# Output blocks inside the arm of a switch, and half-empty blocks in two column tiles: a gated cross-attention and top-4-of-16 MoE kernel on one core

## The chip, the cores and the metric

The kernel runs on one core of a Trainium2 chip. The metric is the device time of one execution in microseconds (us); of several executions the median counts. Everything is computed in 32-bit floats, and a matrix product in this format is recorded as several passes of TensorE (PE). The other engines are VectorE (DVE), ScalarE (ACT), GpSimd (POOL) and the queue that starts most of the loads (SP).

## The reference, cut to what matters

```python
# x: 8 x 256 x 512, ctx: 8 x 256 x 512; LN is a layer norm over the last axis
s   = sigmoid(einsum('bdn,bdm->bnm', LN(x), ctx) / sqrt(256))
x   = x + tanh(g_xattn) * einsum('bvn,bnm->bvm', ctx, s)
xf  = LN(x).reshape(2048, 512)
t   = xf * rsqrt(mean(xf * xf, -1) + eps) * norm_w
vals, idx = top_k(t @ gate_w.T + gate_b, 4)          # 16 experts
G   = zeros(2048, 16); G[row, idx] = softmax(vals)
h   = einsum('mh,eoh->emo', t, w1) + b1              # 1024 outputs: a, b interleaved
a   = minimum(h[..., ::2], 7); b = clip(h[..., 1::2], -7, 7)
act = a * sigmoid(1.702 * a) * (b + 1)
y   = einsum('emi,edi->emd', act, w2) + b2
x   = x + tanh(g_ffn) * (xf + einsum('me,emd->md', G, y))
```

The reference computes all 16 experts for all rows; the kernel computes only the four that a row has chosen.

## The kernel before

The 2048 rows are 16 blocks of 128. The first part (to about 160 us) does attention, norms, the gate and the choice of experts, batch by batch; POOL writes each chosen pair (row, gate) into a table in DRAM, sorted by expert. The second part works on *chunks*: up to R = 4 blocks of 128 rows that all go to one expert. Two early chunks of three blocks (AHEAD) are done while the list of the others is still being built (to about 238 us), and then come the chunks of the list, 22 with these inputs, from 238.2 us to the last pass at 929.6 us.

The list is computed on DVE (lines 905 to 1021), one partition for each block of the list (partition q = 4 * chunk + block). `lim` (L973) is how many rows are left for that block, `full` masks the slots that hold one. `ids` and `gts` (row numbers and gates) are transposed on PE into the PSUM tile `pid` (L991, L992), and copied out as `idsG` (for gathering, L994), `idsT` (for adding to the output, L998; an empty slot gets a number past the last row and is dropped by the bounds check) and `gtsT` (L1000). `meta` holds for each chunk its size class, its number of blocks, its expert and whether it exists.

The order of the work in a chunk is written out by hand (`tc.manual_schedule`), and each engine runs its own instructions in that order. `chunk(c)` (L1108) does:

- POOL gathers the rows of the next chunk (`fetch`, L1037: four indirect loads into xg). The rows of this chunk are in xT already.
- A switch (L1118) over 17 row counts, 256 to 512 in steps of 16. Each of its arms holds `hidden` (L299) for that count: four groups of two PSUM tiles with four products each, recorded as 64 passes, with the row count as the moving size. PE fills `h0` to `h3` in turn (PSUM, four buffers); DVE reads each twice (L308, L317), ACT applies the activation (L316), DVE writes `act` (L325).
- SP loads the first weights of the chunk after the next two (w1r, 2 MB) once hidden has read its slot.
- `turn` (L284, L285): PE transposes the next chunk's rows, 16 passes into four PSUM tiles, and DVE multiplies them by the norm weight into xT.
- `expect` (L1061): PE, DVE and ACT read the next chunk's size class and give a hint at which arm comes next.
- `output` (L1079): block 0 always, blocks 1 to 3 each under an `If` on the number of blocks (L1087). A block is `combine` (L334: eight recorded passes of 512 columns into `h[k]`), the addition of the bias on DVE (L342, yb), the scaling with the gate on ACT (L347, yo), and on POOL an indirect DMA that adds the 128 rows to the output in DRAM (L351). Where a block does not exist, `skip` (L1066) issues four blank products of one column, so that both ways raise the same semaphores.
- SP loads the second weights (w2r) and the output bias (br).

So a chunk with 272 rows computes three full output blocks, though its last one holds 16 rows. The end of an arm (L1213 in the trace) is a jump to the code behind the switch; each arm gives a hint for it at its own start.

Of the kernel before, what the change touches and what calls it, by code (L numbers as in the profile page):

```python
# [31 lines left out]
def kernel(  # L32
# [35 lines left out]
    SIZES = list(range(2 * P, R * P + 1, GRAIN))  # L68
    ROWS = E * NT

    out_rows = out.rearrange("b d n -> (b d) n")

# [26 lines left out]
        "yb": (moe, [P, H], 2),  # L99
        "yo": (moe, [P, H], 3),  # L100
# [33 lines left out]
    blank = const.tile([P, P], mybir.dt.bfloat16, name="blank")  # L134
    nc.vector.memset(blank, 0.0)
# [10 lines left out]
    )  # L146
    eps = const.tile([P, 1], F32, name="eps")
# [69 lines left out]
    for tag in ("xT", "act"):  # L217
        nc.gpsimd.memset(buf(tag, 0), 0.0)
# [110 lines left out]
    def combine(slot, k, lo):  # L329

        py = buf("h", k)
# [9 lines left out]
        yb = buf("yb", k)  # L341
        nc.vector.tensor_tensor(yb, py, br[:, slot, :], ALU.add)  # L342
        return yb

    def scaled(k, yb, gate):
        y = buf("yo", k)
        nc.scalar.activation(y, yb, AF.Copy, scale=gate)  # L347
        return y

    def deliver(c, y, ids):  # L350
        put = nc.gpsimd.indirect_dma_start(  # L351
            out=out_rows,
# [4 lines left out]
            bounds_check=T - 1,  # L357
# [13 lines left out]
    with tc.tile_pool(name="att", bufs=2) as ap:  # L371
# [88 lines left out]
        def second_norm(b):  # L460
# [24 lines left out]
                else buf("yo", c)  # L485
# [267 lines left out]
        def output_early(a):  # L753
            pairs, target = early[a]
            ys = []
            for k in range(AHEAD):
                yb = combine(place_of(a - 2), k, k * P)
                ys.append(scaled(k, yb, pairs[:, k, 1:2]))
            early[a] = ys, target
# [169 lines left out]
    for h in range(2):  # L929
# [45 lines left out]
    )  # L975
    full = small("full", P, P)
# [13 lines left out]
    pid = ps_t.tile([P, 2, P], F32, tag="t", name="pid")  # L990
# [6 lines left out]
    idsT = small("idsT", P, P, dtype=I32)  # L997
    nc.vector.tensor_scalar(idsT, pid[:, 0, :], float(T), None, ALU.add)  # L998
    gtsT = small("gtsT", P, P)
    nc.vector.tensor_copy(gtsT, pid[:, 1, :])  # L1000


    meta = small("meta", P, 4, C1, dtype=I32)
# [9 lines left out]
    nc.vector.tensor_copy(meta[0:1, 1], blocks[0:1])  # L1013
    nc.vector.tensor_copy(meta[0:1, 2], expert[0:1])
    nc.vector.tensor_scalar(
        meta[0:1, 3], unit[0:1], ends[0:1, E - 1 : E], None, ALU.is_lt
# [7 lines left out]
    held_tiles["y"] = [  # L1024
# [7 lines left out]
    held_tiles["x"] = held_tiles["t"] + held_tiles["y"]  # L1032
# [30 lines left out]
    def skip(k):  # L1063

        for i in range(IC):
            nc.tensor.matmul(  # L1066
                buf("h", k)[:, 0:1],
                blank,
                blank[:, 0:1],
                start=True,  # L1070
                stop=True,
            )

    def output_block(c, k):
        q = c * R + k
        yb = combine(place_of(c), k, k * P)
        deliver(c, scaled(k, yb, gtsT[:, q : q + 1]), idsT[:, q : q + 1])

    def output(c):  # L1079


        blocks = read(meta[0:1, 1, c : c + 1], R)
        for k in range(R):
            if k == 0:
                output_block(c, k)
                continue
            with tc.If(blocks > k) as more:  # L1087
                output_block(c, k)
            with more.Else():
                skip(k)  # L1090


    begun = small("begun", P, 4, SLOTS, dtype=I32)
# [14 lines left out]
    def chunk(c):  # L1108
# [5 lines left out]
        e = read(meta[0:1, 2, c : c + 1], E - 1, [ET.DVE])  # L1114
# [102 lines left out]
```

## Time and profile before

| | |
|---|---|
| median of 3 runs | 946.06 us (941.92 to 950.2) |
| profiled execution, its own time | 949.47 us |
| its span | 947.9 us |
| mean granted clock of TensorE | 0.987 |
| 0 to 238 us: PE busy | 214.21 us |
| blocks of output in the list's chunks | 69, and 19 skipped |
| deliveries (L351), mean of one | 69, 1577 ns |

The span is the time from the first to the last instruction in the profile; the profiled execution's own time lies 1.6 us above it. A row of the table of stages has the stretch, its length, then for each engine its busy time and number of instructions, the granted clock, the share of busy DMA engines and GB/s. A row of the waits says which engine and line waited for which, how long in total, how often, and the longest. The chain of waits lists in order of time what ended last: start, length, what. A row of groups has the line, the engine, the operation, what it writes and reads, its shape and count; behind the bar the busy time and the mean of one in ns, the idle time before it and what ended that. A recorded pass lasts longer than the distance to the next one, since passes are pipelined: what a pass costs is read from the chain, as the length of a piece over its count.

### The profile page before, as it was taken

What the parts mean: (1) busy time and instruction counts of PE and PEld (TensorE: products, weight loads), DVE (VectorE), ACT (ScalarE), POOL (GpSimd) and SP (SyncE); (2) the same over time, 40 slices, a digit from 0 to 9 for tenths busy, and PEclk for the clock granted to TensorE, in tenths of its full rate; (3) what the DMA queues carried; (4) which work ended last, traced back from release to release, by engine and by line L of the source; (5) the groups of instructions that cost most, each with busy time, mean ns of one, the idle gap of its engine ahead of it and who ended that gap; (6) DMA issues with size and microseconds to landing.
All of it is one profiled execution on the core that took longest, in us unless ns stands there. A gap on an engine that the chain in (4) does not pass through costs nothing.

```text
span 947.9 us, 10767 instructions
## 1 busy us (share of the span) xinstructions
PE 902.0 (95%) x3134; PEld 524.3 (55%) x3134; DVE 386.1 (41%) x895; ACT 200.5 (21%) x319; POOL 287.6 (30%) x266
## 2 busy tenths in 40 slices
PE   5999995999999999999999999999999999999992
PEld 3455443555555555555444565666667677556760
DVE  3367565584333333333332333333333444333440
ACT  5567662411110110110111110111101111111110
POOL 3034445434230421421312421423213232313222
PEclk9999999999999999999999999999999999999996
DMA  5379942806864545646443654766457667634232
GB/s 170 115 160 166 164 98 69 287 7 154 294 164 159 136 122 167 168 127 192 133 118 117 180 180 128 191 208 187 164 185 216 186 177 210 207 116 123 66 71 32
DMA packets 42339, 144.77 MB, mean 153 GB/s; under 512 B 9569, under 2 KB 9697, under 8 KB 35521
## 3 DMA queue, kind: packets, MB, share of 16 engines
q1 hardware_dynamic: 20016, 98.58, 33.2%
q0 software_dynamic: 20896, 42.96, 20.7%
q8 instruction: 93, 1.52, 0.7%
q14 instruction: 198, 1.61, 0.5%
q10 hardware_dynamic: 1136, 0.10, 0.1%
HBM read 126.33 MB, written 28.38 MB: 163 GB/s over the span
## 4 chain that ended last, share of the span: by engine, by line
PE 60%; issue 14%; DMA 12%; DVE 6%; POOL 3%; ACT 2%; another core or an unknown queue 1%; POOLq 0%; DVEq 0%
PE ph L299 33%; PE ph L334 18%; DMA out_dram<-yo,idsT 11%; PE psc L434 3%; POOL out_dram L351 1%; PE pz L284 1%; PE pt L284 1%; PE pav L446 1%; DVE st L392 1%; DVE xs L453 1%; POOL xg L1037 1%; POOL table L638 1%; ACT xs L509 0%; DVE q L407 0%
## 5 line engine op out<-in xcount | busy, mean ns | idle before, releaser
L299 PE MATMUL ph<-xT,w1r 128*128 128x288 f32 (+10 forms) x1536 | 458.4, 459 | 7.9 <-DVE xT L285 4.7
L299 PEld LDWEIGHTS ph<-xT,w1r 128*128 128x128 f32 x1536 | 291.6, 191 | 166.3 <-issue 66.7
L334 PE MATMUL ph<-w2r,act 128*128 128x512 f32 x600 | 261.6, 592 | 0.6 <-issue 0.5
L351 POOL DMA_INDIRECT out_dram<-yo,idsT x69 | 108.8, 1577 | 461.4 <-ACT yo L347 446.2
L334 PEld LDWEIGHTS ph<-w2r,act 128*128 128x128 f32 x600 | 112.1, 190 | 133.1 <-issue 133.1
L316 ACT ACTIVATE ga<-ga 128x384 f32<-128x384 f32 (+10 forms) x96 | 47.3, 493 | 335.7 <-DVE ga L308 294.9
L317 DVE TENSOR_SCALAR v<-ph,bh 128x384 f32<-128x384 f32 (+10 forms) x96 | 55.6, 579 | 143.2 <-PE ph L299 134.4
L347 ACT ACTIVATE yo<-yb,gtsT 128x512 f32<-128x512 f32 x69 | 47.7, 717 | 293.4 <-DVE yb L342 284.0
L1037 POOL DMA_INDIRECT xg<-t_rows,idsG x92 | 90.7, 985 | 40.0 <-issue 23.0
L308 DVE TENSOR_SCALAR ga<-ph,bh 128x384 f32<-128x384 f32 (+10 forms) x96 | 55.6, 580 | 112.6 <-PE ph L299 83.8
L638 POOL DMA_INDIRECT table<-pair,sloti x64 | 62.5, 977 | 112.7 <-DVE mr L473 79.4
L342 DVE TENSOR_TENSOR yb<-ph,br 128x512 f32<-128x512 f32 x75 | 49.8, 686 | 67.5 <-PE ph L334 43.7
L285 DVE TENSOR_TENSOR xT<-pt,nw 128x512 f32<-128x512 f32 x46 | 29.6, 686 | 111.0 <-issue 97.5
L434 PE MATMUL psc<-kv,q 128*128 128x512 f32 x128 | 60.6, 621 | 2.4 <-ACT kvT L427 2.4
L446 PE MATMUL pav<-sc,kvT 128*128 128x512 f32 x128 | 58.7, 602 | 3.7 <-DVE mine L698 3.4
L325 DVE SCALAR_TENSOR_TENSOR act<-v,ga 128x384 f32<-128x384 f32 (+10 forms) x96 | 50.1, 522 | 14.2 <-ACT ga L316 4.6
L446 PEld LDWEIGHTS pav<-sc,kvT 128*128 128x128 f32 x128 | 23.2, 190 | 31.0 <-issue 26.5
L434 PEld LDWEIGHTS psc<-kv,q 128*128 128x128 f32 x128 | 24.4, 199 | 28.4 <-issue 24.8
L285 DVE TENSOR_TENSOR xT<-pz,nw 128x512 f32<-128x512 f32 x46 | 29.4, 681 | 0.0
L284 PEld LDWEIGHTS pt<-ident,xg 128*128 128x128 f32 x184 | 21.5, 141 | 5.8 <-issue 3.3
L284 PE MATMUL pz<-ident,xg 128*128 128x128 f32 x184 | 23.8, 273 | 0.0
L284 PE MATMUL pt<-ident,xg 128*128 128x128 f32 x184 | 23.8, 273 | 0.0
(177 smaller groups left out, 367.5 us busy)
## 6 DMA issues: line engine op xcount, KB each, us to landing
w1r<-in_L_ffn_w_dram SPq DMA_DIRECT2D x24, 2048.0 KB
w2r<-in_L_ffn_w_dram SPq DMA_DIRECT2D x27, 1024.0 KB
br<-in_L_ffn_b_dram SPq DMA_DIRECT2D x27, 256.0 KB
w1r<-in_L_ffn_w_dram SPq DMA_DIRECT2D x6, 1024.0 KB
xs<-in_x_dram SPq DMA_DIRECT2D x16, 256.0 KB
kv<-in_ctx_dram SPq DMA_DIRECT2D x16, 256.0 KB
out_dram<-xs SPq DMA_DIRECT2D x16, 256.0 KB
t_rows<-u SPq DMA_DIRECT2D x8, 256.0 KB
```

The source lines that it names most:

```text
L284: nc.tensor.transpose(px[:, h, :], xg[:, ts(h, P)], ident)
L285: nc.vector.tensor_tensor(buf("xT", 0)[:, :, lo : lo + P], px, nw.unsqueeze(2).to_broadcast([P, HC, P]), ALU.mult,)
L299: nc.tensor.matmul(ph[:, 0:n], w1r[:, slot, k, h, ts(i, P)], xT[:, k, lo : lo + n], start=(k == 0), stop=(k == HC - 1),)
L308: nc.vector.tensor_scalar(ga[:, 0:n], halves[0][:, 0:n], bias[:, 0, i : i + 1], LIMIT, ALU.add, ALU.min,)
L317: nc.vector.tensor_scalar(v[:, 0:n], halves[1][:, 0:n], bias[:, 1, i : i + 1], 1.0 + LIMIT, ALU.add, ALU.min,)
L325: nc.vector.scalar_tensor_tensor(act[:, i, lo : lo + n], v[:, 0:n], 1.0 - LIMIT, ga[:, 0:n], ALU.max, ALU.mult)
L334: nc.tensor.matmul(py, act[:, i, lo : lo + P], w2r[:, slot, i, :], start=(i == 0), stop=(i == IC - 1),)
L351: put = nc.gpsimd.indirect_dma_start(out=out_rows, out_offset=bass.IndirectOffsetOnAxis(ap=ids, axis=0), in_=y, in_offset=None, compute_op ...
L434: nc.tensor.matmul(ps, qs[b][:, c, ts(n, P)], kvs[b][:, c, :], start=(c == 0), stop=(c == DC - 1),)
L446: nc.tensor.matmul(po, kvTs[b][:, n, ts(c, P)], scs[b][:, n, :], start=(n == 0), stop=(n == NCH - 1),)
L638: put = nc.gpsimd.indirect_dma_start(out=table, out_offset=bass.IndirectOffsetOnAxis(ap=sloti[:, j : j + 1], axis=0), in_=pair[:, c, k, :] ...
L1037: nc.gpsimd.indirect_dma_start(out=buf("xg", k), out_offset=None, in_=t_rows, in_offset=bass.IndirectOffsetOnAxis(ap=idsG[:, q : q + 1], a ...
```

## The change

- The switch's arm now holds more. After hidden come the turn of the next chunk and then `output_rest`: the full blocks 2 and 3, as far as the arm's row count has them, and, if the count in halves of 64 rows is odd, a half block for the last one. Blank products fill up to the same number in every arm. The arm's size decides all of it, so the `If`s and `skip` are gone.
- The half block (`combine_half`) handles 64 rows of `act`. The same 64 rows are the weights of two column tiles: the first makes columns 0 to 255 in partitions 0 to 63, the second columns 256 to 511 in partitions 64 to 127. Its result `yh` (128 x 256) is added to the output seen as rows of half the length.
- After the arm: the load of w1r, the hint, the deliveries of blocks 2 and 3 and of the half block, always, with numbers past the end where there is nothing to add; then blocks 0 and 1 with their deliveries, always.
- The list gets `half` (at most 64 rows left in this block, and it is block 2 or 3), and from it `twice` (the first 64 numbers and gates, doubled), two more transposes into `pid`, `idsH` and `gtsH`; `idsT` leaves out the half blocks. `meta` loses the number of blocks.
- The result tiles `yb` (2) and `yo` (3) become `y` (4) and `yh` (1), scaled in place. `blank` is a view of `ones`.

```diff
@@ -66,9 +66,11 @@
 
     GRAIN = 16
     SIZES = list(range(2 * P, R * P + 1, GRAIN))
+    HALF = P // 2
     ROWS = E * NT
 
     out_rows = out.rearrange("b d n -> (b d) n")
+    out_halves = out.rearrange("b d (g n) -> (b d g) n", g=2)
 
     const = ctx.enter_context(tc.tile_pool(name="const", bufs=1))
     ring = ctx.enter_context(tc.tile_pool(name="ring", bufs=1))
...
@@ -96,8 +98,8 @@
         "act": (moe, [P, IC, R * P], 1),
         "ga": (moe, [P, R * P], 2),
         "v": (moe, [P, R * P], 2),
-        "yb": (moe, [P, H], 2),
-        "yo": (moe, [P, H], 3),
+        "y": (moe, [P, H], R),
+        "yh": (moe, [P, H // 2], 1),
     }
     held_tiles = {
         tag: [pool.tile(shape, F32, name=f"{tag}{i}") for i in range(n)]
...
@@ -131,8 +133,8 @@
     make_identity(nc, ident)
     ones = const.tile([P, P], F32, name="ones")
     nc.gpsimd.memset(ones, 1.0)
-    blank = const.tile([P, P], mybir.dt.bfloat16, name="blank")
-    nc.vector.memset(blank, 0.0)
+
+    blank = ones.bitcast(mybir.dt.bfloat16)[:, 0:P]
 
     ahead = const.tile([P, P], F32, name="ahead")
     nc.gpsimd.affine_select(
...
@@ -144,6 +146,10 @@
         base=0,
         channel_multiplier=-1,
     )
+
+    behind = const.tile([P, 1], F32, name="behind")
+    nc.gpsimd.memset(behind[0:HALF], 2.0 * T)
+    nc.gpsimd.memset(behind[HALF:P], 2.0 * T + 1.0)
     eps = const.tile([P, 1], F32, name="eps")
     nc.gpsimd.memset(eps, EPS)
     eps2 = const.tile([P, 1], F32, name="eps2")
...
@@ -326,9 +332,8 @@
             act[:, i, lo : lo + n], v[:, 0:n], 1.0 - LIMIT, ga[:, 0:n], ALU.max, ALU.mult
         )
 
-    def combine(slot, k, lo):
-
-        py = buf("h", k)
+    def combine(slot, py, y, lo, gate):
+
         act = buf("act", 0)
         for i in range(IC):
             nc.tensor.matmul(
...
@@ -338,23 +343,39 @@
                 start=(i == 0),
                 stop=(i == IC - 1),
             )
-        yb = buf("yb", k)
-        nc.vector.tensor_tensor(yb, py, br[:, slot, :], ALU.add)
-        return yb
-
-    def scaled(k, yb, gate):
-        y = buf("yo", k)
-        nc.scalar.activation(y, yb, AF.Copy, scale=gate)
-        return y
-
-    def deliver(c, y, ids):
+        nc.vector.tensor_tensor(y, py, br[:, slot, :], ALU.add)
+        nc.scalar.activation(y, y, AF.Copy, scale=gate)
+
+    def combine_half(slot, py, y, lo, gate):
+
+
+        act = buf("act", 0)
+        for i in range(IC):
+            for g in range(2):
+                nc.tensor.matmul(
+                    py[ts(g, HALF), 0 : H // 2],
+                    act[:, i, lo : lo + HALF],
+                    w2r[:, slot, i, ts(g, H // 2)],
+                    start=(i == 0),
+                    stop=(i == IC - 1),
+                )
+        for g in range(2):
+            nc.vector.tensor_tensor(
+                y[ts(g, HALF)],
+                py[ts(g, HALF), 0 : H // 2],
+                br[ts(g, HALF), slot, ts(g, H // 2)],
+                ALU.add,
+            )
+        nc.scalar.activation(y, y, AF.Copy, scale=gate)
+
+    def deliver(c, y, ids, rows=out_rows):
         put = nc.gpsimd.indirect_dma_start(
-            out=out_rows,
+            out=rows,
             out_offset=bass.IndirectOffsetOnAxis(ap=ids, axis=0),
             in_=y,
             in_offset=None,
             compute_op=ALU.add,
-            bounds_check=T - 1,
+            bounds_check=rows.shape[0] - 1,
             oob_is_err=False,
         )
         for other in added.setdefault(c, []):
...
@@ -754,8 +775,8 @@
             pairs, target = early[a]
             ys = []
             for k in range(AHEAD):
-                yb = combine(place_of(a - 2), k, k * P)
-                ys.append(scaled(k, yb, pairs[:, k, 1:2]))
+                ys.append(buf("y", AHEAD * a + k))
+                combine(place_of(a - 2), buf("h", k), ys[k], k * P, pairs[:, k, 1:2])
             early[a] = ys, target
 
         def deliver_early(a, k):
...
@@ -973,6 +994,12 @@
     nc.vector.scalar_tensor_tensor(
         lim, part, -float(P), rows[:, mine], ALU.mult, ALU.add
     )
+
+    half = small("half", P, 1)
+    nc.vector.tensor_scalar(half, lim, float(HALF), None, ALU.is_le)
+    late = small("late", P, 1)
+    nc.vector.tensor_scalar(late, part, 2.0, None, ALU.is_ge)
+    nc.vector.tensor_tensor(half, half, late, ALU.mult)
     full = small("full", P, P)
     nc.vector.tensor_scalar(full, upto, lim, None, ALU.is_lt)
 
...
@@ -987,20 +1014,43 @@
     )
     gts = small("gts", P, P)
     nc.vector.tensor_tensor(gts, got[:, :, 1], full, ALU.mult)
-    pid = ps_t.tile([P, 2, P], F32, tag="t", name="pid")
+
+    twice = got.rearrange("p s c -> p (s c)").rearrange("p (c s) -> p c s", c=2)
+    pid = ps_t.tile([P, 4, P], F32, tag="t", name="pid")
     nc.tensor.transpose(pid[:, 0, :], ids, ident)
     nc.tensor.transpose(pid[:, 1, :], gts, ident)
     idsG = small("idsG", P, P, dtype=I32)
     nc.vector.tensor_scalar(
         idsG, pid[:, 0, :], float(T), float(T - 1), ALU.add, ALU.min
     )
-    idsT = small("idsT", P, P, dtype=I32)
-    nc.vector.tensor_scalar(idsT, pid[:, 0, :], float(T), None, ALU.add)
     gtsT = small("gtsT", P, P)
     nc.vector.tensor_copy(gtsT, pid[:, 1, :])
-
-
-    meta = small("meta", P, 4, C1, dtype=I32)
+    for h, some in enumerate((ids, gts)):
+        nc.vector.tensor_scalar(
+            twice[:, h].rearrange("p (g s) -> p g s", g=2),
+            some[:, 0:HALF].unsqueeze(1).to_broadcast([P, 2, HALF]),
+            half,
+            None,
+            ALU.mult,
+        )
+        nc.tensor.transpose(pid[:, 2 + h, :], twice[:, h], ident)
+
+    two = small("two", P, P)
+    nc.vector.tensor_copy(two, pid[:, 2, :])
+    idsT = small("idsT", P, P, dtype=I32)
+    nc.vector.scalar_tensor_tensor(
+        idsT, pid[:, 0, :], float(T), two, ALU.add, ALU.subtract
+    )
+    idsH = small("idsH", P, P // R, dtype=I32)
+    gtsH = small("gtsH", P, P // R)
+    ends2 = two.rearrange("p (c k) -> p k c", k=R)
+    nc.vector.tensor_tensor(gtsH, ends2[:, R - 2], ends2[:, R - 1], ALU.add)
+    nc.vector.tensor_scalar(idsH, gtsH, 2.0, behind, ALU.mult, ALU.add)
+    nc.vector.tensor_copy(two, pid[:, 3, :])
+    nc.vector.tensor_tensor(gtsH, ends2[:, R - 2], ends2[:, R - 1], ALU.add)
+
+
+    meta = small("meta", P, 3, C1, dtype=I32)
     larger = rough[0][:, 0 : C1 * (len(SIZES) - 1)].rearrange("p (c s) -> p c s", c=C1)
     nc.vector.tensor_tensor(
         larger[0:1],
...
@@ -1010,10 +1060,9 @@
     )
     nc.vector.tensor_reduce(gap[0:1], larger[0:1], AX.X, ALU.add)
     nc.vector.tensor_copy(meta[0:1, 0], gap[0:1])
-    nc.vector.tensor_copy(meta[0:1, 1], blocks[0:1])
-    nc.vector.tensor_copy(meta[0:1, 2], expert[0:1])
+    nc.vector.tensor_copy(meta[0:1, 1], expert[0:1])
     nc.vector.tensor_scalar(
-        meta[0:1, 3], unit[0:1], ends[0:1, E - 1 : E], None, ALU.is_lt
+        meta[0:1, 2], unit[0:1], ends[0:1, E - 1 : E], None, ALU.is_lt
     )
     toti = small("toti", P, 1, dtype=I32)
     nc.vector.tensor_copy(toti[0:1], ends[0:1, E - 1 : E])
...
@@ -1021,7 +1070,7 @@
     hidden_early(1, 3)
     inorder.close()
 
-    held_tiles["y"] = [
+    held_tiles["z"] = [
         ps_y.tile([P, HC, P], F32, tag="y", name=f"pz{i}") for i in range(2)
     ]
     held_tiles["t"] = [
...
@@ -1029,7 +1078,7 @@
     ]
 
 
-    held_tiles["x"] = held_tiles["t"] + held_tiles["y"]
+    held_tiles["x"] = held_tiles["t"] + held_tiles["z"]
 
 
     def fetch(c, k):
...
@@ -1060,37 +1109,34 @@
 
         tc.switch_hint(size_of(c), len(SIZES), label=f"size_{c}")
 
-    def skip(k):
-
-        for i in range(IC):
-            nc.tensor.matmul(
-                buf("h", k)[:, 0:1],
-                blank,
-                blank[:, 0:1],
-                start=True,
-                stop=True,
-            )
-
     def output_block(c, k):
         q = c * R + k
-        yb = combine(place_of(c), k, k * P)
-        deliver(c, scaled(k, yb, gtsT[:, q : q + 1]), idsT[:, q : q + 1])
-
-    def output(c):
-
-
-        blocks = read(meta[0:1, 1, c : c + 1], R)
-        for k in range(R):
-            if k == 0:
-                output_block(c, k)
-                continue
-            with tc.If(blocks > k) as more:
-                output_block(c, k)
-            with more.Else():
-                skip(k)
-
-
-    begun = small("begun", P, 4, SLOTS, dtype=I32)
+        py = buf("h", k + 2)
+        combine(place_of(c), py, buf("y", k), k * P, gtsT[:, q : q + 1])
+
+    def output_rest(c, halves):
+
+        for k in range(2, halves // 2):
+            output_block(c, k)
+        if halves % 2:
+            k = halves // 2
+            combine_half(
+                place_of(c), buf("h", k + 2), buf("yh", 0), k * P, gtsH[:, c : c + 1]
+            )
+
+
+        blocks = max(0, halves // 2 - 2)
+        for _ in range(3 * IC - blocks * IC - halves % 2 * 2 * IC):
+            nc.tensor.matmul(
+                buf("h", 3)[:, 0:1], blank, blank[:, 0:1], start=True, stop=True
+            )
+
+    def deliver_block(c, k):
+        q = c * R + k
+        deliver(c, buf("y", k), idsT[:, q : q + 1])
+
+
+    begun = small("begun", P, 3, SLOTS, dtype=I32)
 
     def meta_of(c):
         return begun if c < SLOTS else meta
...
@@ -1099,8 +1145,8 @@
 
         if c not in held:
             held[c] = (
-                read(meta_of(c)[0:1, 3, c : c + 1], 1, [ET.SP]),
-                read(meta_of(c)[0:1, 2, c : c + 1], E - 1, [ET.SP]),
+                read(meta_of(c)[0:1, 2, c : c + 1], 1, [ET.SP]),
+                read(meta_of(c)[0:1, 1, c : c + 1], E - 1, [ET.SP]),
             )
         go, e = held[c]
         load(e, c, cond=go)
...
@@ -1111,20 +1157,27 @@
         if c + 1 < MAXC:
             for k in range(R):
                 fetch(c + 1, k)
-        e = read(meta[0:1, 2, c : c + 1], E - 1, [ET.DVE])
+        e = read(meta[0:1, 1, c : c + 1], E - 1, [ET.DVE])
         nc.vector.tensor_copy(
             bh[:, c % 2], b1s[:, bass.ds(e, 1)].rearrange("p o s c -> p (o s) c")
         )
         for i in tc.Switch(size_of(c), len(SIZES), hint=f"size_{c}"):
             for n in range(IC):
                 hidden(place_of(c), bh[:, c % 2], n, 0, SIZES[i])
+            if c + 1 < MAXC:
+                for k in range(R):
+                    turn(k, buf("x", k), k * P)
+            output_rest(c, -(-SIZES[i] // HALF))
         if c + SLOTS < MAXC:
             bring(c + SLOTS, load_hidden, held)
         if c + 1 < MAXC:
-            for k in range(R):
-                turn(k, buf("x", k), k * P)
             expect(c + 1)
-        output(c)
+        for k in range(2, R):
+            deliver_block(c, k)
+        deliver(c, buf("yh", 0), idsH[:, c : c + 1], out_halves)
+        for k in range(2):
+            output_block(c, k)
+            deliver_block(c, k)
         if c + SLOTS < MAXC:
             bring(c + SLOTS, load_output, held)
```

More of the change, by code (lines that the diff above doesn't have):

```diff
@@ L215 @@
     )
-    for tag in ("xT", "act"):
+    for tag in ("xT", "act", "yh"):
         nc.gpsimd.memset(buf(tag, 0), 0.0)
@@ L484, in second_norm @@
                 if b % 2 == 0
-                else buf("yo", c)
+                else buf("y", c)
                 for c in range(DC)
```

## The prediction

> **What bounds the kernel now.** I read the page's first two parts, then the table of stages, then the waits of the chunk stage, then the chain of waits over a long and a short chunk. First the page:
>
> ```profile
> span 947.9 us, 10767 instructions
> PE 902.0 (95%) x3134; PEld 524.3 (55%) x3134; DVE 386.1 (41%) x895; ACT 200.5 (21%) x319; POOL 287.6 (30%) x266
> ```
>
> The stage table splits the span at the first chunk of the list and after the last pass:
>
> ```profile
> 238.00:948.00 710.00, 687.80 (x2389) 411.85 (x2387) 250.33 (x444) 91.57 (x158) 197.51 (x159) 0.99 0.55 157
> 929.60:947.90 18.30, 0.00 (x0) 0.00 (x0) 0.65 (x1) 0.72 (x1) 1.55 (x1) 0.60 0.18 26
> ```
>
> From 238.2 to 929.6 TensorE works for 687.8 of 691.4 us at a granted clock of 0.99: only fewer or cheaper passes shorten this stage, and a stall lengthens it one for one. The 18.3 us of tail hold no pass. The waits of this stage, for PE and for the engine that feeds it:
>
> ```profile
> PE ph L299 <- DVE yb L342: 3.1, 3, 1.2
> PE ph L334 <- issue: 0.5, 1, 0.5
> DVE xT L285 <- issue: 97.5, 18, 5.9
> ```
>
> PE waits 3.6 us in all. DVE waits 5.4 us on average, 18 times, before its first addition behind an arm, with nothing to wait for: the arm's end is a jump, and its code is late. PE makes the same jump and shows nothing. The chain over the first chunk (448 rows) and over the short one at 604 (256 rows):
>
> ```profile
> 238.37 24.05 PE ph L299 x64
> 262.43 0.87 PE pt L284 x8
> 263.30 0.87 PE pz L284 x8
> 264.17 13.73 PE ph L334 x32
> ```
>
> ```profile
> 604.36 13.81 PE ph L299 x64
> 618.18 0.87 PE pt L284 x8
> 619.05 0.87 PE pz L284 x8
> 619.92 3.45 PE ph L334 x8
> 623.37 1.36 issue
> 624.73 0.43 DVE xT L285
> ...
> 627.13 0.69 DVE yb L342
> ```
>
> A full output block is 13.73 / 4 = 3.43 us, the turn 1.74 us, and PE goes from the arm into the turn without a gap. In the short chunk DVE's late jump (xT at 624.73) delays the yb that frees a PSUM buffer: this is the 3.1 us above. How often each size occurs, at 64 passes a chunk:
>
> ```profile
> L299 PE MATMUL ph<-xT,w1r 128*128 128x288 f32 x256 | 63.0, 407 | 1.2 <-DVE yb L342 1.2
> L299 PE MATMUL ph<-xT,w1r 128*128 128x256 f32 x256 | 56.2, 380 | 0.0
> L299 PE MATMUL ph<-xT,w1r 128*128 128x448 f32 x128 | 48.5, 540 | 0.0
> L299 PE MATMUL ph<-xT,w1r 128*128 128x400 f32 x128 | 43.3, 499 | 0.0
> L299 PE MATMUL ph<-xT,w1r 128*128 128x272 f32 x128 | 29.9, 394 | 1.9 <-DVE yb L342 1.9
> L299 PE MATMUL ph<-xT,w1r 128*128 128x416 f32 x64 | 22.5, 512 | 0.0
> L299 PE MATMUL ph<-xT,w1r 128*128 128x320 f32 x64 | 17.5, 434 | 0.0
> ```
>
> Sizes whose last block holds at most 64 rows are 272, 288, 320, 400, 416 and 448: 2 + 4 + 1 + 2 + 1 + 2 = 12 chunks of 22. Four have 256; of the other six, 336, 368 and twice 384 have three full blocks, and 480 (twice) four.
>
> **Part 1: the half block.** In 12 chunks 8 passes of 512 columns (3.43 us) become 16 passes of 256 columns into two column tiles. The only column tiles in the trace are the gate's (four of them, over 128 rows of contraction, 256 columns):
>
> ```profile
> 113.90 1.72 PE psc L434 x4
> 115.62 0.57 PE pl L539 x8
> ```
>
> Eight such passes in a row would take 8 x 0.216 = 1.73 us (0.216 is the hidden pass at 256: 13.81 / 64); they take 0.57, so tiles do run beside each other, as two sets of four, 0.43 us, plus 0.14 us for going in and out. The half block is eight sets of two: 8 x 0.216 + 0.14 = 1.87 us. Bounds: 1.73 (nothing for going in and out) and 16 x 0.216 = 3.46 (no overlap). I take 1.87, since the gate's row has the same contraction and the same columns. Gain: 12 x (3.43 - 1.87) = **-18.7 us**; bounds -20.4 and +0.4.
> [...]
>
> **Part 2: the turn and the later blocks go into the arm, the Ifs go.** The passes are the same, in another order: after the turn the later blocks, then behind the jump blocks 0 and 1.
> (a) DVE's xT now comes before its late jump, so PE's 3.1 us go: **-3.1** (0 to -3.1). Next late on DVE: with 256 rows it leaves the arm about 4.5 us after hidden's last pass (act about 1.6, four xT at 0.69), its jump of 5.4 brings it to 9.9, two y additions to 11.5, and the next arm's code by about 14 (its sequencer's rows have it 5.3 us or less after the hint in short chunks). PE wants the first PSUM pair back after turn, two blocks and two of four hidden groups: 1.74 + 6.87 + 6.9 = 15.5. A thin 1.5 us; with a half block PE's side grows more than DVE's. Cost 0.
> (b) PE's own jump. Before, 18 pairs of long hidden passes are queued when PE's sequencer reaches it (its rows show it 3.45 us ahead of the turn in 256-row chunks), so a late target is covered; even the code fetched after the jump lands too late (another 1.4 us until usable, by its packets) to explain that the turn starts on time, so the target was there. Afterwards the queue holds blanks, a half block or part of the turn: by the same 18 pairs 1.0 us with 256 rows, 2.0 with five halves, 4.1 with six, 2.7 with seven, 6 with eight. After the jump come two register loads, some moves and the hint, 1.1 to 1.4 us in the rows of before. If the code is there, only the four 256-row chunks can see this: 4 x 0.5 = **+2** (0 to 2).
> (c) The switch. Before, PE's hint preceded two to four blocks; now always two, 6.87 us. In the short chunk at 604 its rows have the hint at 618.74 and the arm running at 626.39, 7.65 us, while 2 MB of w1r are landing. With a hint later than that load's first microseconds it should be less, and before the load it is covered. Between 0 and 0.8 us a chunk; I take 0.2 x 21 = **+4** (0 to 17).
> (d) Blanks: 12 x 4 + 4 x 7 + 8 x 4 + 0 x 5 + 4 x 2 = 116 against 76 before, at 0.02 to 0.04 us: **+1**.
> (e) POOL now issues 5 deliveries a chunk, 110 against 69, at 1.58 us, less 19 skips of 1.5 us: +36 us, covered by its 450 us of waiting for yo. Without the cover the next fetch would come late for the turn; a chunk needs some 13 us of POOL and lasts 23 or more. The half and later blocks are delivered before blocks 0 and 1, and the order of the last two at the end, so the 18.3 us of tail stay. SP's load of w1r still waits only for hidden. ACT scales in place: the same count. Cost 0.
>
> **Part 3: the list.** PE waited 1.67 us for ids and restarted at 215.84. Two more transposes now wait for idsG, gtsT and two multiplications on DVE (0.28 to 0.29 us each, 0.2 us apart, from 216.04): hidden restarts at about 217.2: **+1.4** (0.6 to 3). Some ten small DVE operations (2.5 us) lie beside the 8.55 us of hidden passes that follow; the first fetch moves by nothing, as idsG keeps its place.
>
> **Sum** against the profiled execution (949.47 us; span 947.9, with 1.6 us around it): -18.7 - 3.1 + 2 + 4 + 1 + 1.4 = -13.4, so 936. That execution is 3.4 us above the median of 946.06: the forecast is **933 us**.
>
> **Rivals.**
> A, slower: PE's jump behind the arm is late, as DVE's is. Place: between the arm and block 0, each chunk. For it: the 97.5 us of DVE, under the same hint, ACT likewise; the arm on PE is nearly twice as long, with less in the queue. Against it: PE showed no such wait. Price where it happens: 5.4 + 1.2 less the queued work of (b): 5.6 x 4 + 4.6 x 7 + 2.5 x 4 + 3.9 x 5 + 0.6 x 2 = 85 us, so 1018; in a third of the chunks +28, 961. It decides from 13.4 / 22 = 0.6 us a chunk on.
> [...]
> B: the two column tiles do not overlap. The gain of 18.7 goes: 949.5 - 3.1 + 2 + 4 + 1 + 1.4 = 955, less 3.4, 951. The gate's 0.57 us speak against it.
> C: (c) at its upper end, and (b) with it: +13 on the forecast, 946. For it: the 7.65 us; against it: the load's burst is over sooner after the longer arms.
>
> **How the numbers follow.** Forecast (925 to 941, its own range): 0.54; C and lesser stalls (941 to 955): 0.16; A (955 to 1018): 0.25; B: 0.05. The range 922 to 985 leaves out the upper half of A and little below. One per cent, 9.5 us, is about what can be told from no change here: faster is below 936.6, some eight tenths of the forecast's case and a little of C, 0.46; slower is above 955.5, A and some of B, 0.27; the rest, 0.27, is within.
>
> **What would show it.** Half blocks of 16 passes in 1.9 us, with the next block right behind; no PE wait for yb; a hidden restart near 217; PE busy down by some 16 us and its idle time in the chunk stage below 10. Wrong: an "issue" gap of PE before block 0 (A) or before hidden (C), 3.4 us per half block (B), or PE waiting for DVE in hidden's third group, where my 1.5 us were too thin.

## The result, and the profile after

| | before | after |
|---|---|---|
| median of 20 runs each | 946.34 us (940.6 to 955.71) | 936.67 us (928.05 to 946.18) |
| ratio after / before | | 0.9865, 95% interval 0.9838 to 0.9893 |
| profiled execution, its span | 949.47, 947.9 us | 941.34, 939.7 us |
| first pass of the list's chunks to last pass | 691.3 us | 684.3 us |

The ratio is taken over the undisturbed runs alone, those at most 1.5% above the fastest of their kernel; the two medians as they stand give 0.9898. On 946.3 us it is 12.8 us less, 10.1 to 15.3. The forecast was 933, 13.4 less. The two profiled executions differ by only 8.1 us, and that of after lies 4.7 us above its own median; part of the reason comes out below.

The page of after, and its stage table for the chunks and for the tail (stretch, length, then each engine's busy time and number of instructions, granted clock, share of busy DMA engines, GB/s):

```profile
span 939.7 us, 10479 instructions
PE 891.5 (95%) x3272; PEld 520.6 (55%) x3272; DVE 383.6 (41%) x915; ACT 199.6 (21%) x319; POOL 350.3 (37%) x310
```

```profile
238.00:948.00 710.00, 676.75 (x2528) 408.13 (x2526) 246.96 (x456) 90.64 (x158) 260.53 (x200) 0.99 0.55 158
923.50:939.70 16.20, 0.02 (x1) 0.00 (x0) 0.69 (x1) 0.72 (x1) 3.08 (x2) 0.66 0.34 44
```

PE has 11 us less to do in the chunk stage, at the same mean clock. The tail is 2.1 us shorter. The chain of waits over the first chunk, and the timeline of VectorE around the start of the 288-row chunk that follows one of 480:

```profile
239.42 24.05 PE ph L305 x64
263.48 0.87 PE pt L290 x8
264.35 0.87 PE pz L290 x8
265.22 3.44 PE ph L339 x8
268.66 1.88 PE ph L355 x16
270.54 7.06 PE ph L339 x16
```

```profile
533.30 0.69 DVE L346 TENSOR_TENSOR y<-ph,br 128x512 f32<-128x512 f32 x1 [2.61 <-PE ph L339]
533.91 0.16 DVE L1161 COPY bh<-b1s 128x8 f32 x1
542.49 0.52 DVE L314 TENSOR_SCALAR ga<-ph,bh 128x288 f32<-128x288 f32 x1 [8.41 <-issue]
```

The first shows the half block (L355): 16 passes in 1.88 us, where a full block took 3.43. The second shows what went wrong: VectorE is idle for 8.41 us before the first operation of its new arm, and "issue" says that it waited for nothing that the profile shows. Between the switch's jump at 534.45 and 542.3, though, two packets of 8 KB land on queue 14 and one of 16 KB on queue 8, both of the kind that the profile calls instruction. So it is in all 18 chunks with more than 256 rows: two or three packets of queue 14 between the jump and the first ga. In the four with 256 rows there is none, and in the kernel before none in 19 of 22 chunks. These packets and the runs below are why the waits are here put down to code; for which engine a packet is, the profile does not say. TensorE starts that chunk at 533.10, runs two of its four groups, and then stands (stretch by stretch, in the form of the stage table):

```profile
533.10:541.10 8.00, 7.92 (x33) 5.89 (x31) 0.77 (x2) 0.72 (x1) 6.25 (x6) 1.00 0.85 209
543.06:546.55 3.49, 3.49 (x8) 2.50 (x9) 2.13 (x5) 0.89 (x2) 0.00 (x0) 0.51 0.62 228
```

Behind the stand of 2.03 us the granted clock is 0.51 for 3.5 us, and 8 passes take the time of 14. The waits of PE in the chunk stage of after, and VectorE's; the first line is the kernel before, for comparison:

```profile
DVE ga L308 <- issue: 28.7, 16, 6.8
DVE ga L314 <- issue: 65.0, 9, 8.5
DVE y L346 <- issue: 33.0, 6, 5.9
PE ph L305 <- DVE ga L314: 6.2, 6, 2.0
PE ph L339 <- DVE xT L291: 1.6, 4, 0.5
PE ph L305 <- issue: 0.5, 1, 0.5
PE ph L305 <- DVE y L346: 0.4, 1, 0.4
```

PE's waits for yb (3.1 us before) are nearly gone, and 6.2 us of waits for ga have come. They are not the whole of it: a recorded pass of 288 rows lasts 0.41 us and the next starts 0.24 us after it, so each of the six waits costs some 0.17 us more than its row says, 1.0 us in all (an estimate from these two numbers); and the half clock behind the longest, at 543.06, costs another 1.7 us (six passes at 0.48 us instead of 0.24, and part of the one before them). The 65.0 us are not the whole of VectorE's lateness either: of the 18 chunks with more than 256 rows nine are in that line, and in the other nine VectorE is idle for 5.4 to 7.9 us as well, which the profile puts down to TensorE's product because that came last by its records. From the start of each chunk to that of the next, summed over kinds of chunk:

| chunks | before to after | of which |
|---|---|---|
| 6 with a half block and 320 to 448 rows | -8.3 us | about -1.4 each |
| 6 with a half block and 272 or 288 rows | -0.1 us | -8.2 expected from the others; hidden passes stretched by 9.2, 1.1 of yb's waits gone |
| 4 with 256 rows | +0.5 us | yb waits gone; new small waits and blanks |
| 6 without a half block, over 320 rows | +0.8 us | blanks, 0.1 to 0.2 each |
| sum | -7.1 us | |

### The profile page after: what moved, and what is told of

It is laid out like the page before. It is cut to its first block, busy times and chain, and to the rows that moved or that the text cites. A ratio compares the mean times of both kernels' runs of the same rounds, so it can differ in the third digit from the quotient of the medians.

```text
span 939.7 us, 10479 instructions
## 1 busy us (share of the span) xinstructions
PE 891.5 (95%) x3272; PEld 520.6 (55%) x3272; DVE 383.6 (41%) x915; ACT 199.6 (21%) x319; POOL 350.3 (37%) x310
## 4 chain that ended last, share of the span: by engine, by line
PE 76%; issue 10%; DMA 7%; POOL 3%; DVE 3%; ACT 1%; DVEq 0%; POOLq 0%; SPq 0%
PE ph L305 40%; PE ph L339 20%; PE psc L455 4%; PE pav L467 4%; PE ph L355 2%; DMA xs<-in_x_dram 2%; DMA out_dram<-y,idsT 2%; POOL out_dram L372 2%; DMA out_dram<-xs 2%; PE pz L290 2%; PE pt L290 2%; POOL table L659 1%; DVE xT L291 1%; PE pkv L445 1%; DMA gx_raw<-in_g_xattn_dram 0%
## 5 line engine op out<-in xcount | busy, mean ns | idle before, releaser
L372 POOL DMA_INDIRECT out_dram<-y,idsT x88 | 137.9, 1567 | 391.6 <-ACT yh L369 206.8
L339 PE MATMUL ph<-w2r,act 128*128 128x512 f32 x504 | 223.8, 596 | 1.6 <-DVE xT L291 1.6
L339 PEld LDWEIGHTS ph<-w2r,act 128*128 128x128 f32 x504 | 92.9, 190 | 107.6 <-issue 103.6
L346 DVE TENSOR_TENSOR y<-ph,br 128x512 f32<-128x512 f32 x63 | 43.0, 690 | 151.8 <-PE ph L339 103.0
L347 ACT ACTIVATE y<-y,gtsT 128x512 f32<-128x512 f32 x57 | 40.7, 721 | 231.4 <-DVE y L346 231.4
L467 PE MATMUL pav<-sc,kvT 128*128 128x512 f32 x128 | 62.1, 632 | 3.5 <-DVE mine L719 3.1
L372 POOL DMA_INDIRECT out_dram<-yh,idsH x22 | 34.0, 1546 | 8.3 <-issue 4.6
L413 DVE BATCH_NORM_STATS2 st<-xs 128x6 f32<-128x512 f32 x32 | 21.9, 685 | 11.6 <-DMA xs<-in_x_dram 11.0
```

The lines of the kernel that those rows point to most:

```text
L339: nc.tensor.matmul(py, act[:, i, lo : lo + P], w2r[:, slot, i, :], start=(i == 0), stop=(i == IC - 1),)
L372: put = nc.gpsimd.indirect_dma_start(out=rows, out_offset=bass.IndirectOffsetOnAxis(ap=ids, axis=0), in_=y, in_offset=None, compute_op=ALU ...
L467: nc.tensor.matmul(po, kvTs[b][:, n, ts(c, P)], scs[b][:, n, :], start=(n == 0), stop=(n == NCH - 1),)
```

## The experiments

All kernels differ from the changed kernel by the edit shown, unless the text says "the kernel before". "Stage" is the time from the first pass of the list's chunks to the last pass in the profile (691.3 before, 684.3 after). "Wait for the arm" is the median time, in VectorE's rows, from the switch's jump to the first ga of its arm, over all chunks but the first and those with 256 rows: 0.9 us before, 7.2 us after. Span and stage come from one profiled execution each; a ratio is to the kernel before on the same chip.

**What is the half block worth?** The last block is computed in full, everything else is kept (`half` is never set):

```diff
-        for k in range(2, halves // 2):
+        blocks = max(0, -(-halves // 2) - 2)
+        for k in range(2, 2 + blocks):
             output_block(c, k)
-        if halves % 2:
...
```

> The changed kernel with its half block computed as a full block inside the arm (the same order, no Ifs, the same list operations). First theory: a half block costs 2.07 us on PE (two full-block chunks differ by 1.36 us before and after the change) and the new order costs about 9 us because VectorE finds its next arm's code late. Then each of the 12 chunks gets 1.36 us longer, 16 us in all: about 953 against 936.7, and the kernel lies some 6 us above the kernel before. Rival: the order costs nothing and the half blocks alone made the difference: then it lands at the kernel before, within 2 us.

Measured: 957.42 us, ratio 1.0101 (1.0071 to 1.013), stage 698.9. Without half blocks the change is a loss of about 10 us (6 were expected); the half blocks are worth 1.0101 - 0.9865, some 22 us between the two ratios and 14.6 us between the two profiled stages (the profiled execution of after is a dear one, in part by its half clock). The rival is out: the new order does cost.

**Do the two column tiles overlap?**

```diff
-        for i in range(IC):
-            for g in range(2):
+        for g in range(2):
+            for i in range(IC):
                 nc.tensor.matmul(
                     py[ts(g, HALF), 0 : H // 2],
```

> The changed kernel, with the half block's two loops swapped: all four products of the first column tile, then all four of the second. If the tiles run beside each other only when consecutive passes go to different tiles, the 16 passes take 16 x 0.216 = 3.46 us instead of 1.88, and the profiled span grows by 12 x 1.6 = 19 us. Rival: tiles overlap in any order, or the passes have been serial all along: the span stays within 3 us.

Measured: span 948.4, stage 694.0. The first chunk takes 39.09 us from start to start against 38.18, so a half block costs 0.91 us more: some 2.8 us for 16 passes against 1.88. So the two tiles' passes overlap more when they alternate, 1.88 us against 2.8. Both expectations missed the size: 12 x 0.91 = 11 us, not 19, as 16 passes take 2.8 and not 3.46 us even tile by tile; why they do is not shown.

**Does the late code cost the 9 us, and can the hint be given earlier?** VectorE's and ScalarE's hint for the next switch goes to the end of the arm, in front of the jump:

```diff
             output_rest(c, -(-SIZES[i] // HALF))
+            if c + 1 < MAXC:
+                expect(c + 1, [ET.DVE, ET.Activation])
...
-            expect(c + 1)
+            expect(c + 1, [ET.PE])
```

> The changed kernel, with the hint of VectorE and ScalarE for the next switch given as the last thing in the arm instead of behind the jump; TensorE's stays where it is. First theory: after the switch VectorE waits up to 8.5 us for its arm's code because the hint comes too late or is lost behind the jump; given earlier the code is there, PE's hidden groups of the 272- and 288-row chunks go back from 16.4 to 19.5 us to about 15, and 7 to 9 us go: about 928. Rival: VectorE is late because it has more to do before the switch, or because only code that lies right behind the jump is ever there, hint or not: no change, within 2 us of 936.7.

Measured: 931.34 us, ratio 0.9827 (0.98 to 0.9854), stage 675.1. The same place in the timeline of this kernel:

```profile
532.11 0.69 DVE L346 TENSOR_TENSOR y<-ph,br 128x512 f32<-128x512 f32 x1 [2.21 <-PE ph L339]
532.72 0.16 DVE L1163 COPY bh<-b1s 128x8 f32 x1
534.22 0.52 DVE L314 TENSOR_SCALAR ga<-ph,bh 128x288 f32<-128x288 f32 x1 [1.34 <-PE ph L305]
```

The 8.41 us are gone, and VectorE waits for a product again. PE's waits in the chunk stage of this kernel, and VectorE's for nothing before ga:

```profile
PE ph L339 <- DVE xT L291: 1.2, 3, 0.4
PE ph L305 <- DVE y L346: 0.7, 1, 0.7
PE ph L305 <- issue: 0.5, 1, 0.5
PE ph L339 <- issue: 0.4, 1, 0.4
DVE ga L314 <- issue: 12.2, 9, 6.3
```

PE has no wait for ga left, the 288-row chunks take 26.3 us instead of 27.1 to 30.3, and the wait for the arm is 1.5 us (VectorE's 6.3, in the last line, is the first chunk's). Only the place of the hint has changed, so the lateness is one of code, and it is worth 9.2 us of the stage in these two profiles.

A second time, on another chip:

> The kernel with the hint inside the arm once more, on another chip, to see how much of the 9 us that its profile gains in the chunk stage shows in executions without a profile. If the late code costs as much there as under the profile, the ratio to the kernel before is 0.977 or less; if the profile makes the fetches dearer than they are without it, the ratio is about 0.983 as the first time, some 4 us below the changed kernel's 0.9865.

Measured: 925.64 us, ratio 0.982 (0.9789 to 0.9851), stage 674.3. Between ratios the gain on the changed kernel is about 4 us, half of what the two profiles show. The next runs tell part of the reason: with the same late code their stages are 681.4 and 680.2 instead of 684.3, so that the lateness costs 5 to 9 us from execution to execution. No wait of PE in their chunk stages is longer than 1.8 us; 1.7 us of the 9.2 are the half clock that the changed kernel's profile caught. Whether profiling itself makes the fetches dearer is open.

**Is it the load that makes the fetch slow?** The second load goes behind the next chunk's first:

```diff
             bring(c + SLOTS, load_hidden, held)
+        if c > 0 and c - 1 + SLOTS < MAXC:
+            bring(c - 1 + SLOTS, load_output, brought[c - 1])
+        brought[c] = held
...
-        if c + SLOTS < MAXC:
-            bring(c + SLOTS, load_output, held)
```

> The changed kernel, with each chunk's second load (w2r and bias, 1.3 MB) issued not at the end of the chunk but in the next chunk, right after the load of w1r. First theory: VectorE's arm code after the switch is fetched while this load fills the DMA engines, which makes 7 us out of 3.6 (the one such wait in the last chunks, where nothing is loaded, is 3.6); without the load there PE's stretched hidden groups go back and 5 to 9 us are saved: about 929. Against it, the jump at the arm's end now meets the longer load and may take 2 us more. Rival: the lateness has nothing to do with the load: within 2 us of 936.7.

Measured: 933.66 us, ratio 0.9843 (0.9817 to 0.987), stage 675.9. The wait for the arm is 3.2 us, for every size but 256, instead of 7.2: the code is still late, but with the load moved it is there in less than half the time. As expected, the other jump got dearer; PE waited no longer for it, but 1.3 us, in two places, stand against the later load of br. VectorE's waits in the chunk stage:

```profile
DVE y L346 <- issue: 81.0, 15, 5.9
DVE ga L314 <- issue: 51.0, 17, 6.7
```

(y is the first operation behind the arm's jump: 81.0 us against 33.0.) With 3.2 us VectorE is in time for TensorE's third group, and PE's stretched groups are gone. The time fell less than the stage and than expected: the interval covers the changed kernel's 0.9865.

**Does the hint do anything where it stands?** First the changed kernel, then the kernel before, each with `expect(c + 1, [ET.PE])` alone:

> The changed kernel without any hint of VectorE and ScalarE for the next switch (TensorE keeps its own). Theory: behind the jump these hints do nothing: VectorE finds its code only when the next chunk has 256 rows (the first arm, right behind the jump's code) and waits about 7 us otherwise, just as in the changed kernel; span 939.7 within 3 us. Rival: the hints do help and are only too late by a part: then the waits get longer than 7 us and the span grows by 5 us or more.

Measured: span 940.5, stage 681.4, wait for the arm 7.2 us (0.8 with 256 rows): as with the hint. In the changed kernel it does nothing.

> The kernel before without the hint of VectorE and ScalarE for the next switch (TensorE keeps its own). If the hint worked there, VectorE now waits about 4 to 7 us after each switch jump instead of 0.8, except for the 256-row chunks, and PE's groups of the 272- and 288-row chunks are stretched as in the changed kernel: span up by 3 to 9 us from 947.9. If code read ahead in order had been enough there, nothing changes: within 2 us.

Measured: span 955.7, stage 696.6 (+5.3), wait for the arm 6.3 instead of 0.9 us. VectorE's and PE's waits in its chunk stage:

```profile
DVE ga L308 <- issue: 74.7, 17, 7.3
PE ph L299 <- DVE ga L308: 1.5, 1, 1.5
```

So in the kernel before the same hint worked, and without it that kernel has the same fault.

**What made the hint fail?** Four runs. The hint given later, after block 0's addition and scaling (`if k == 0 and c + 1 < MAXC: expect(c + 1, [ET.DVE, ET.Activation])` in the loop over blocks 0 and 1):

> The changed kernel with the hint of VectorE and ScalarE given after block 0's addition and scaling, not right behind the jump; TensorE's stays. If the hint is lost because it comes within 0.7 us of the jump's landing, this one is taken, a fetch follows it, and the waits after the switch fall from 7 us where at least 4 us are left before it (chunks after 384 rows and more); the span falls by up to 5 us. Rival: it is the time before the switch that counts: then it is worse or the same, 939 to 943.

Measured: span 942.5, stage 680.2, wait for the arm 7.2 us: this hint is lost as well. It is not that it came too soon behind the jump; that too little time is left before the switch, the other reading, stands so far.

The kernel before with the turn inside the arm, Ifs and full blocks kept:

```diff
                 hidden(place_of(c), bh[:, c % 2], n, 0, SIZES[i])
+            if c + 1 < MAXC:
+                for k in range(R):
+                    turn(k, buf("x", k), k * P)
```

> The kernel before with only the turn of the next chunk moved into the arm, the Ifs and the full blocks as they were. Theory: PE's three waits for yb behind 256-row chunks go (3.1 us), and VectorE's hint now follows the jump as closely as in the changed kernel, so it is lost as there: long waits after the switch except before 256-row chunks, but with two to four blocks under Ifs between hint and switch; span 945 to 950. Rival: the hint works as before, and the span falls by 3 us to 944 to 945.

Measured: span 949.6, stage 689.0 (-2.3; the first part of this execution was 4.6 us longer), wait for the arm 1.0 us. The hint works, though it comes as early behind the jump as in the changed kernel: my theory of that moment fell. PE's waits for yb went from 3.1 to 1.9 us; most of the expected 3 us came.

What is left of the difference are the Ifs, with the time that they take. Block 1 and its delivery are put under one that is always true:

```diff
-        for k in range(2):
-            output_block(c, k)
-            deliver_block(c, k)
+        output_block(c, 0)
+        deliver_block(c, 0)
+        with tc.If(used > c):
+            output_block(c, 1)
+            deliver_block(c, 1)
```

> The changed kernel with block 1 and its delivery put under an If that is always true, so that a branch lies again between VectorE's hint and its switch; the hint stays right behind the arm's jump, and the time between hint and switch stays. Theory: a hint is followed up only at a next branch or jump that is not the hinted one (in the kernel before the Ifs were that, with the hint in the arm it is the jump). Then the waits after the switch fall from 7 to 1 or 2 us and the time to about 931, less if the branches cost TensorE some tenths a chunk. Rival: it was the time under the Ifs, or the shorter arms, that made the hint work before: then the waits stay at 7 us and the time at 936 or a little above.

Measured: 934.77 us, ratio 0.9889 (0.9846 to 0.9931), stage 677.5, wait for the arm 3.9 us, in one chunk of 400 rows 6.5 and in one of 256 rows 6.6. The hint works again, half: not 1 to 2 us as expected. Why only half is not shown: VectorE's rows have 2.0 to 5.8 us between this branch and the switch's jump, the waits hardly follow it, and in the kernel before 4.0 us were enough for waits of 0.8 to 1.1. The time did not fall with the stage: its interval covers the changed kernel's ratio.

That time alone makes a hint work is ruled out by the first chunk of the list. Its hint is given 10.4 to 10.7 us before its jump in every one of these kernels, with no branch between, and VectorE waits 6.0 to 7.2 us there, in the kernel before as well (hint at 229.2, jump at 239.6):

```profile
239.09 0.16 DVE L1115 COPY bh<-b1s 128x8 f32 x1
246.08 0.68 DVE L308 TENSOR_SCALAR ga<-ph,bh 128x448 f32<-128x448 f32 x1 [6.83 <-issue]
```

The next chunk of 448 rows there has its hint 7.2 us before its jump, with Ifs between, and waits 0.8 us. And the Ifs without a hint do not help either: that is the 6.3 us of the kernel before without it.

The arms in reverse order (512 rows first):

> The changed kernel with the switch's arms in reverse order, 512 rows first and 256 last. Theory: without a working hint VectorE has its code only if the arm lies right behind the jump's code: now the chunks of 480 rows (third arm) start without the 7 us wait and the four with 256 rows have it. Rival: the 256-row chunks were spared because of what goes before them or because their arm is short: then they stay spared and 480 keeps its 7 to 8 us.

Measured: span 951.0, stage 693.0. Three of the four 256-row chunks now wait 6.9 to 7.2 us (the fourth, at the end with no loads, 3.2), and PE's passes of such a chunk stretch from 13.6 to 17.9 us at worst. So 256 rows were spared because their arm came first. But 480 rows, now the third arm, still wait 7.3.

**Both remedies** (the hint in the arm, and the later load):

> The changed kernel with both remedies: the hint of VectorE and ScalarE as the last thing in the arm, and the second load issued after the next chunk's first load. Theory: either one already takes away PE's waits for VectorE (7 to 9 us), so both together give no more than one: 929 to 932. Rival: what is left of the lateness still costs, and the two add up: 925 or below.

Measured: 929.99 us, ratio 0.9858 (0.9823 to 0.9892), stage 675.9, as with either alone. They do not add. The kernel to keep is the one with the hint in the arm: 0.9827 and 0.982 in two measurements. Each of their intervals still overlaps the changed kernel's 0.9838 to 0.9893 a little, so that the gain rests on the two together and on the profiles.

## Why the prediction was right, and where it was not

The time, the sign and the range held: 933 forecast, 936.67 measured. The sum held partly because errors cancel, and one step failed.

- **The half block, right.** Forecast 1.87 us, measured 1.88 in the chain. Taking the price from the gate's four column tiles was sound. Behind it, blocks 0 and 1 take 7.06 instead of 6.87 us (the chain's 16 passes), so that a long chunk gains 1.36 us net. Of this 0.19, some 0.1 is also there in chunks without a half block. So beyond the 0.14 us in the sum a half block costs about 0.1 us in the blocks behind it, 1 us in all. PE's busy time in the chunk stage fell by 11 us and not by the 16 looked for; with the hint in the arm it fell by 15.5. Over eight sets at 0.216 us the half block and what stands behind it cost 1.88 - 1.73 and the 0.1, some 3 us over 12; that this is for going in and out of the tiles is the prediction's reading of the gate's row, and no run shows it.
- **(a) VectorE, wrong.** The prediction had VectorE's arm code ready 5.3 us or less after the hint, as in the short chunks of before, and its lead over PE's third group as "a thin 1.5 us", at a cost of 0. The hint no longer worked; the first ga came 7.2 us after the switch's jump and some 8.5 us after TensorE's first pass, and the step cost 9.2 us in the profiled execution (5 to 9 over three): 6.2 of PE standing before hidden's third group, 1.7 of half clock, an estimated 1.0 in the passes around the waits, and 0.3 without a source. The error was to carry over a hint's row without what lay between hint and switch: the Ifs that the change takes away (Ifs and hint 0.9 us; hint alone 7.2, Ifs alone 6.3). The sign to look for had been named, though ("PE waiting for DVE in hidden's third group").
- **The 3.1 us of yb, right in kind.** The turn's move alone gives 2.3 of them. In the changed kernel the 256-row chunks are 0.5 us longer all the same: it was turned into new waits.
- **(b) PE's jump.** Forecast 0.5 us for each of the four 256-row chunks, measured 0.34 to 0.47. But what PE waits for there is VectorE's xT, not its own register loads. Rival A, with PE's code late behind the arm, is refuted: PE's sequencer passes the jump at the arm's end in 0.30 to 0.36 us in every chunk, while VectorE stands behind it six times, 33.0 us in all. Why the one finds its code there and the other does not is not shown; at the jump into an arm, under (c), PE's code is late too.
- **(c) PE's switch: late, but covered.** Forecast +4, measured 0.5 (PE's one wait for "issue", before a chunk of 272 rows). PE's code was late all the same. The jumps in its sequencer's rows, before and after (shortest, median and longest in ns, those into the arms and those at their ends together):

```profile
L1213 PEldq COMPARE_BRANCH  x44: 300/342/3297, 231.2 to 912.4; - x44
L1266 PEldq COMPARE_BRANCH  x44: 299/456/6572, 232.5 to 914.5; - x44
```

Of the 22 jumps into an arm 19 now take 3.3 to 6.6 us, against 0.3 to 3.3 before. In each of the 19 a 16 KB packet of the kind instruction lands on queue 8, and the jump ends 1.3 to 1.6 us later. The passes of blocks 0 and 1, 6.9 us, are queued meanwhile and hide it, with only 0.2 us to spare in three chunks. So PE's switch was late as feared, and only the price of 0.2 us a chunk was too high; whether PE's hint is lost too or only comes too late was not tried. Rival C is out. Rival B is refuted by the 1.88 us.

- **(d) Blanks**: 0.1 us for four; as forecast.
- **The list**: PE's second wait, 0.78 us, and two transposes bring hidden's restart 1.3 us later (forecast 1.4).
- **The tail**: forecast unchanged, measured 16.2 against 18.3 us; the three kernels whose blocks are skipped under Ifs have 17.7 to 18.3 and all others 15.6 to 16.3. Where a block is skipped, POOL still spends 1.5 us on it (the 19 skips of the prediction), and the last chunk ends with a skipped one; that this is the cause was not tried.

In the profile: -18.6 (half blocks) + 2.3 (0.19 x 12) + 9.2 (late code) + 0.0 (all else: yb's 3.1 us and what the 256-row chunks and the blanks gave back) = -7.1 for the stage; the tail -2.1; the list begins 1.05 us later; sum -8.1. That the median fell further, by 9.7, and the ratio by 12.8, fits with the late code's cost of 5 to 9 us, and with a profiled execution at its upper end; that part is argued, not shown.

## What to carry to other kernels

Where a step takes away branches, time an engine off the critical path from its last jump to its first operation behind the next, and not by its load: here that went from 0.9 to 7.2 us on VectorE, busy for 41% of the span both before and after. Lines in the profile that name "issue" as what an engine waited for need not cost anything: VectorE's 97.5 us before xT cost TensorE 3.1 us in the kernel before; its 65.0 us before ga came where TensorE was two groups from needing it, and there the lateness cost 5 to 9 us. An engine with work queued can have code just as late and show nothing: TensorE's jumps took up to 6.6 us here, behind 6.9 us of queued passes, and only its sequencer's rows show them. For a block of output rows that is half empty, two column tiles with alternating passes took 1.88 us here instead of 3.43; the row of another column-tiled product with the same contraction and the same columns was enough to forecast it.

## What the runs showed that was not expected

- On VectorE and ScalarE a hint for a switch did nothing when no other branch or jump lay between it and the switch (wait 7.2 us with it, 7.2 without it, 7.2 when it was given later), and worked when one did: Ifs 0.9 to 1.0 us, one If 3.9, the arm's own jump 1.5. The first chunk's hint, over 10 us early with no branch between, did nothing in any kernel (6.0 to 7.2). That it is the branch is the one reading that fits all these kernels; how it comes about, and why one If gave only half, is not shown.
- TensorE's passes hardly waited for code in these kernels (0.5 us for "issue" before hidden in the kernel after), but its sequencer did: its jump into an arm has a median of 0.8 to 0.9 us in the three kernels with blocks under Ifs, and of 2.9 to 5.3 us in all others.
- A stand of TensorE of 2.03 us in the middle of the kernel after's chunk stage was followed by 3.5 us at a granted clock of 0.51. In the run with the arms reversed so were stands of 2.33 and 2.21 us, while one of 2.21 us in the run with one If was not; what brings the lower clock on is not shown.
- VectorE's wait for the arm was 7.2 us beside a load of 1.3 MB, and 3.2 us with that load moved.
- The list's first pass came at 235.8 to 246.1 us in profiled executions of kernels whose first part is nearly the same: much of the scatter of the metric lies there and has nothing to do with the change.
